# A two-layer kernel with per-sample weights and adapters: when the second layer's weight sums, adapters and next weights are made

## The chip, the cores and the metric

The kernel runs on one core of one Trainium2 chip. The time is device microseconds from launch to end, as the chip reports it for that core. The profile adds one traced execution. Its span, from the first to the last instruction, is somewhat shorter than the time of the same execution. Engines: PE (matmul), PEld (weight loads of PE), DVE (VectorE), ACT (ScalarE), POOL (GpSimd), and SP, which here only issues DMAs. DMAs are also issued from the queues of ACT and POOL.

## The reference

The input x is 8 batches of 256 tokens with 1024 features, in float32. Two layers follow, each with a residual.

```
# layer 1: per batch b a 0/1 mask of 1024 x 1024 and a coefficient c[b]
x = x + (x @ W0.T + b0) + (x @ (2*mask[b] - 1)) * c[b]
# layer 2: per batch b one of 24 adapters, rank 16, scaling 2
x = x + (x @ W1.T + b1) + 2 * (x @ A[itok[b]]) @ B[itok[b]]
```

## The kernel before, in words

**Layer 1.** A batch's effective weight is W0.T + 2c*mask - c, with the identity added for the residual. It is made in pieces of 128 x 1024 float32, eight to a batch, numbered k = 8b + i. `load(k)` issues the DMA of the mask (512 KB) and, for half of the pieces, of an x tile (256 KB) on SP's queue (L203, L207). `build(k)` expands the mask on ACT (L231) and adds W0 on DVE (L234). Batches 0 to 2 multiply the pieces directly (L292, L267). Batches 3 to 7 (`Seven`) cut weights and tokens into halves and do seven products in place of eight. `operands` makes the pieces, the weight sums s1 to s4 (L345) and the token sums t1 to t4 (L362); `products` multiplies (L408), adds the bias on ACT (L423) and accumulates quarters on DVE (L428). Its banks X, Y and Z are PSUM tiles.

**Layer 2.** It works on groups of four batches, and `second_layer` runs once after batch 3 and once after batch 7. The seven-product scheme is used at two levels. The outer products are A11, A12, S1, S2, S4, S3 and A22, in this order (`plan`), and `run` does one. Each has seven inner products with the leaves a11, s1, s2, a12, s3, a22 and s4 of 256 KB (L695). A leaf is read from DRAM by SP (L685) into one of seven buffers, each as soon as a buffer is free. The tiles e1 and e5 hold outer products that are needed twice, and c11, c12, c21 and c22 are the output quarters. `read` takes a finished bank out of PSUM: with a seed by a DVE add (L750), without one by an ACT copy (L749). The products A11 and S1 have no seed, so they are the ones that use ACT copies. ACT's queue also issues the stores of the output (L754). The adapters come in as `down` (L730, into h_sb), and `up` (L713, banks G), copied out by ACT (L723).

**W1's leaves.** W1 is loaded as 16 tiles of 256 KB (`raw`). `combine_weights` makes the sums of A11, A12, S1 and so on out of them in batches 2 and 3, by DVE, and `keep` (L514) stores each leaf to DRAM from POOL's queue. What doesn't fit then is left as generators in `later`: A22's four inner sums (L552 to L558), S2's four, S4's four, made in place (L575), and S3, which first reads two quarters back from DRAM on POOL's queue (`again`, L594, eight DMAs), then makes four outer sums (L586) and four inner ones in place. In batch 3 the hook `mid`, after the product s1, starts the adapters (`begin_adapters`: two DVE copies, two POOL memsets, eight DMAs on POOL's queue; `load_adapters`: another DVE copy and eight DMAs), then makes A22's sums and issues the stores of three of S4's quarters. The hook `late`, after s3, makes S2's sums. S4's and S3's sums come in the second layer.

**What sets the order.** A planner orders each engine's instructions when the program is built. It follows the order of the program, but by its own estimate of times it lets an instruction that is ready go ahead of an earlier one that is not. On the chip every engine then works through its list in that order. `behind(name)` restricts the planner: an instruction in its block is placed after the one kept as `anchors[name]`, if it runs on the same engine. "reads" is the last DVE read of a bank, "leaves" the last leaf load on SP, "weights" the last weight sum, "rows" the last adapter DMA on POOL. `run` takes a generator `beside` of small DVE steps (one step at each of four points, the rest at its end): the token sums of later products, the left weight sums, and, in group 0, the first pieces of batch 4 (`next_weights`, through `begin`). `next_masks(n)` issues the loads of batch 4's first n pieces.

**Buffers.** "w" has six tiles of 512 KB (pieces of even batches and of batch 1, the sums of A22 and S2, S3's A21), "q" ten (W1's quarters, e and c tiles), "l" seven (the leaves).

Of the kernel before, what the change touches and what calls it, by code (L numbers as in the profile page):

```python
# [24 lines left out]
def kernel(  # L25
# [38 lines left out]
    nc = tc.nc  # L64
# [105 lines left out]
    def load(k: int):  # L170

        b, h, g = pieces[k]

        if b in SEVEN and k % (2 * NG) >= 6 and b >= GB:
            pool, tag = qpool, "q"
        elif b in SEVEN and b % 2 and k % (2 * NG) < 6:
            pool, tag = tpool, "T"
        else:  # L180
            pool, tag = wpool, "w"
        weff[k] = pool.tile([P, CG, OH], F32, tag=tag, name=f"w_{k}")
        last = (k + 1) % (GB * 2 * NG) == 0
        pairs = [(weff[k].bitcast(I32), mask[b, g if b == 0 else h * NG + g])]
        if b == 0:
            pairs.append((w0_of(k), w0T[g]))
        x_pair = g // CG if b == 0 and g % CG == 0 else g if h == 0 else None
        if x_pair is not None:
            x = x_sb[b, x_pair] = xpool.tile([P, CG, T], F32, tag=f"x{x_pair}", name=f"x_{b}_{x_pair}")
        if k < BY_HALF:  # L190

            for i in range(2):
                for t, a in pairs:
                    nc.sync.dma_start(t[:, i], part(a, i))  # L194
                if k == 0 and i == 0:
                    nc.scalar.dma_start(x[:, 0], part(xT[0, 0], 0))
                elif k == 0:
                    nc.sync.dma_start(x[:, 1], part(xT[0, 0], 1))
                elif x_pair is not None and i == 0:
                    nc.sync.dma_start(x, xT[b, x_pair])  # L200
        else:
            for t, a in pairs:
                sent = nc.sync.dma_start(t, a)  # L203
            if last:
                anchors["masks"] = sent
            if x_pair is not None:
                nc.sync.dma_start(x, xT[b, x_pair])  # L207
        if k == NG:
            nc.sync.dma_start(b0_sb, b0)
        if k == 2 * NG:  # L210
            nc.sync.dma_start(itok_sb, itok)
        for n, (q, r) in enumerate(W1_ORDER):
            if k == 0 and r % 2 == 0:
                two = pair(f"w1_{q}_{r // 2}")
                raw[q, r], raw[q, r + 1] = two[:, 0], two[:, 1]
            if k == 2 * NG + n // 2:
                nc.sync.dma_start(raw[q, r], w1T[q, r])

    def build(k: int):
# [98 lines left out]
    class Seven:  # L318
# [3 lines left out]
        def __init__(self, b: int):  # L322
            self.b = b
            self.w, self.t = {}, {}
            self.ps = {}
            self.mid = self.late = lambda: None

        def block(self, i, j, a):

# [87 lines left out]
        def out(self, i, v):  # L417
            return self.y[i][:, :, v * H : (v + 1) * H]

        def with_bias(self, i, v, ps):  # L420
            for j in range(TPH):
                ot = i * TPH + j
                nc.scalar.activation(  # L423
                    self.out(i, v)[:, j, :], ps[:, j, :], AF.Identity, bias=b0_sb[:, ot : ot + 1]
                )
# [4 lines left out]
        def products(self):  # L430

            ps = self.ps
            for a in range(2):
                self.half("X", "a11", (0, 0), a, first=True)
                yield
            self.with_bias(0, 0, ps["X"])
            for a in range(2):
                self.half("Y", "a12", (1, 0), a, first=True)
                yield

            with behind("weights") if self.b < GB else nullcontext():
                self.add(0, 0, ps["Y"])
            for a in range(2):
                self.half("X", "s2", "t2", a)
                yield
            self.with_bias(0, 1, ps["X"])
            for a in range(2):
                self.half("Z", "s1", "t1", a, first=True)
                yield
            self.with_bias(1, 1, ps["Z"])  # L450
            self.mid()
            for a in range(2):
                self.half("X", "s3", "t3", a)
                yield
            self.add(1, 1, ps["X"])
            self.late()
            for a in range(2):
                self.half("Z", "s4", (1, 1), a)
                yield
            self.add(0, 1, ps["Z"])  # L460
            for a in range(2):
                self.half("X", "a22", "t4", a)
                yield
            self.with_bias(1, 0, ps["X"])
# [5 lines left out]
    def behind(what: str):  # L470
        return tc.issue_after(anchors[what].ins) if what in anchors else nullcontext()

    class Sevens:
# [6 lines left out]

        def begin(self, early: int):
            while self.made < early:
                with behind("reads"):
                    next(self.operands, None)
                self.made += 1

# [31 lines left out]
    def combine_weights():  # L518
# [17 lines left out]
        def inner(name, blocks, own, spare=False):  # L536


            a11, a12, a21, a22 = (blocks[u, v] for u in range(2) for v in range(2))
            for n, t in (("a11", a11), ("a12", a12), ("a22", a22)):  # L540
                if n in own:
                    keep(name, n, t)
            s = {}
            for n in ("s1", "s2", "s3", "s4"):
                if not spare:
                    s[n] = lpool.tile([P, CG, OQ], F32, tag="l", name=f"{name}_{n}")
                else:
                    if n in ("s1", "s3"):
                        half = wpool.tile([P, 2, CG, OQ], F32, tag="w", name=f"{name}_{n}")
                    s[n] = half[:, n in ("s2", "s4")]  # L550
                if n == "s1":
                    nc.vector.tensor_add(s[n], a21, a22)  # L552
                elif n == "s2":
                    nc.vector.tensor_sub(s[n], s["s1"], a11)
                elif n == "s3":
                    nc.vector.tensor_sub(s[n], a11, a21)
                else:
                    nc.vector.tensor_sub(s[n], a12, s["s2"])  # L558
                keep(name, n, s[n])
                yield  # L560
# [112 lines left out]
    def second_layer(group: int, y, first, first_steps, second):  # L673
# [72 lines left out]

        def read(out, ps, other=None):
            if other is None:
                return nc.scalar.copy(out, ps)  # L749
            own["reads"] = anchors["reads"] = nc.vector.tensor_add(out, ps, other)  # L750
            return anchors["reads"]

# [101 lines left out]
                if group + 1 < NGROUP:  # L854
                    load_to((group + 1) * GB * 2 * NG + n)

        def next_weights():
            for n in range(3 if group + 1 < NGROUP else 0):
                sevens[group + 1].begin(n + 1)
                yield  # L860


        def ordered(steps):
# [5 lines left out]
                yield  # L869

        own = {}
        left = {n: ordered(later[n] if group == 0 else iter(())) for n in ("S3", "S4")}
        with behind("masks"):
            load_leaves("A11")
        begin(0, "A11", first)
        for _ in ordered(first_steps):
# [3 lines left out]
        lower = (c11, c12)  # L880
        run(
            0, "A11", first, None, e1,
            beside=chain(ordered(second.sums()), islice(left["S3"], 1), islice(t1, 2), left["S4"]),
            early=down,
            mid=lambda: up(0, 0, lower),
            late=lambda: up(0, 1, lower),
# [2 lines left out]
        for uv in UV[1:]:  # L889
            add(c11[uv], e1[uv])  # L890
        t2 = ordered(outer_sum(2, b22, big_t[1], "S2"))
        run(
            1, "A12", second, c11, c11,
            dest=(0, 0),
            beside=chain(t1, islice(left["S3"], 4), islice(t2, 2)),
        )
        next_masks(4)
        e5 = quads("e5")
        run(
            2, "S1", right["S1"], None, e5,  # L900
            beside=chain(t2, ordered(right["S4"].sums()), left["S3"]),
            then=lambda uv: add(c12[uv], e5[uv]),
        )
        run(
# [6 lines left out]
        run(  # L911
            4, "S4", right["S4"], c12, c12,
            dest=(0, 1),
            beside=ordered(outer_sum(4, b21, big_t[2], "A22")),
            mid=lambda: up(1, 0, upper),
            late=lambda: up(1, 1, upper),
        )
# [5 lines left out]
                    add(c22[uv], e5[uv])  # L923
                yield

        nonlocal limit
        limit = n_pieces
        run(5, "S3", right["S3"], e1, e1, beside=chain(next_weights(), add_e5()), then=lambda uv: add(c21[uv], e1[uv]))


        next_masks(6)
# [5 lines left out]
                yield  # L937

        run(6, "A22", right["A22"], c21, c21, dest=(1, 0), beside=last_quarter())


    load_to(LOADS_AHEAD)
# [8 lines left out]
    def step(k: int):  # L951

        nonlocal sums
        if k == 2 * NG + 1:
            sums = combine_weights()
        with tc.issue_after(weff_at[min(k + BUILDS_AHEAD, max(weff_at))].ins):
            for _ in range(3):
# [5 lines left out]
    for group in range(NGROUP):  # L963
# [18 lines left out]
        if group == 0:  # L982
# [3 lines left out]
            for _ in sums:  # L986
                pass

            def mid(late=y[GB - 1][1][:, 0, H : H + 1]):
                with behind("weights"):  # L990
                    begin_adapters(late)
                    load_adapters(0, late)
                sums_of("A22")
                with behind("rows"):
                    next(later["S4"])

            def sums_of(name):
                with behind("weights"), behind("rows"):
                    for _ in later[name]:
                        pass  # L1000

            sevens[0].batches[-1].mid = mid
            sevens[0].batches[-1].late = lambda: sums_of("S2")
        sevens[group].run(y, between)
        anchors["layer"] = anchors["weights"]
        second_layer(group, y, first, first_steps, second)
# [72 lines left out]
```

## Time and profile before

| | us |
|---|---|
| time, median of 3 runs | 417.87 (416.04, 417.87, 525.24) |
| time of the profiled execution | 416.53 |
| its span | 414.4 |
| PE busy | 403.4 (97%) |
| DVE busy | 312.0 (75%) |
| ACT busy | 137.5 (33%) |
| POOL busy | 42.8 (10%) |
| DMA | 99.55 MB, 240 GB/s on the mean |

The stages by PE in the trace: batch 3 from 90.4 to 115.4 us, group 0's second layer from 115.4 to 217.4, batches 4 to 7 from 217 to 317.3 (their first matmuls are mixed into A22's), and group 1's second layer from 317.3 to the end. The table's shares are means over stages with different limits. A line of the timeline reads: start, length, engine, line, operation, output<-input, shapes, count, and in brackets how long the engine was idle before and what ended that. A line of the waits reads: who waited for whom, us in total, how often, the longest.

### The profile page before, as it was taken

The page shows a single profiled execution, that of the slowest core. Times are in us where ns is not written, and L with a number is a line of the kernel's source. Part 1 is how long each engine was busy: PE and PEld are TensorE (multiplying, and loading weights), DVE is VectorE, ACT ScalarE, POOL GpSimd, SP SyncE. Part 2 cuts the span into 40 slices and gives each one's busy share as a digit, 9 for nine tenths or more (in the row PEclk, how much of TensorE's full clock was granted, in tenths as well). Part 3 has the DMA queues.
Part 4 walks back from the last instruction along what each step waited for, and adds up shares of the span by engine and source line. Part 5 has one row for each costly group of instructions (what it writes and reads, how often), then busy time and mean ns, then how long its engine had stood idle before and what let it go on. Part 6 is the DMA issues. An engine that isn't in the chain of part 4 may idle for free.

```text
span 414.4 us, 6761 instructions
## 1 busy us (share of the span) xinstructions
PE 403.4 (97%) x2554; PEld 358.7 (87%) x2554; DVE 312.0 (75%) x446; ACT 137.5 (33%) x221; POOL 42.8 (10%) x85
## 2 busy tenths in 40 slices
PE   8999999999999978999998999999999999999996
PEld 6888888899977866888888999999999788888885
DVE  3357598889704985997999999999922177898593
ACT  4443434872134105013037864732221420101100
POOL 0000252000784210200000000300000000000000
PEclk9999999999999998999999999999999999999999
DMA  8999999960389999766699857732113247655654
GB/s 289 405 402 395 402 412 418 408 269 2 98 294 365 320 315 405 242 195 226 209 358 396 317 160 251 272 121 58 27 52 74 80 127 236 171 154 158 220 156 152
DMA packets 42403, 99.55 MB, mean 240 GB/s; under 512 B 5636, under 2 KB 6404, under 8 KB 42372
## 3 DMA queue, kind: packets, MB, share of 16 engines
q1 hardware_dynamic: 32690, 76.17, 53.3%
q0 software_dynamic: 4928, 14.71, 9.5%
q10 hardware_dynamic: 4754, 8.26, 5.4%
q8 instruction: 20, 0.33, 0.3%
q14 instruction: 11, 0.09, 0.1%
HBM read 79.19 MB, written 19.92 MB: 239 GB/s over the span
## 4 chain that ended last, share of the span: by engine, by line
PE 90%; DMA 4%; DVE 2%; ACT 1%; issue 1%; SPq 1%; DVEq 0%; ACTq 0%
PE X L695 24%; PE X L408 17%; PE ps L267 12%; PE Z L695 11%; PE Z L408 9%; PE Y L695 5%; PE ps L292 4%; PE Y L408 3%; PE G L713 2%; PE psh L730 2%; DMA outT<-c 2%; DMA w_sb<-w0T 2%; DMA w<-mask 1%; DVE w L234 1%; SPq L194 1%
## 5 line engine op out<-in xcount | busy, mean ns | idle before, releaser
L231 ACT ACTIVATE w<-w,neg_c,two_c 128x1024 f32<-128x1024 int32 (+1 forms) x67 | 79.9, 1203 | 72.6 <-DMA w<-mask 45.8
L234 DVE TENSOR_TENSOR w<-w,w_sb 128x1024 f32<-128x1024 f32 (+1 forms) x67 | 77.3, 1172 | 24.6 <-ACT w L231 21.3
L267 PE MATMUL ps<-x,w 128*128 128x256 f32 x256 | 55.7, 379 | 0.3 <-DVE w L234 0.3
L267 PEld LDWEIGHTS ps<-x,w 128*128 128x128 f32 x256 | 48.6, 190 | 7.2 <-DVE w L234 0.7
L423 ACT ACTIVATE y<-X,b_sb 128x128 f32<-128x128 f32 x60 | 17.1, 367 | 61.8 <-PE X L408 60.5
L833 DVE TENSOR_TENSOR c<-c,e 128x512 f32<-128x512 f32 x48 | 31.9, 684 | 5.4 <-ACT c L723 4.6
L408 PE MATMUL X<-t,s 128*128 128x128 f32 x288 | 33.9, 275 | 1.1 <-ACT y L423 1.1
L723 ACT COPY c<-G 128x512 f32<-128x512 f32 x32 | 16.4, 600 | 54.7 <-PE G L713 54.7
L408 PEld LDWEIGHTS X<-t,s 128*128 128x128 f32 x288 | 33.0, 192 | 1.3 <-ACT y L423 1.3
L292 PE MATMUL ps<-x,w 128*128 128x256 f32 x128 | 28.2, 381 | 0.5 <-DVE w L234 0.5
L292 PEld LDWEIGHTS ps<-x,w 128*128 128x128 f32 x128 | 24.3, 191 | 4.6 <-DVE w L234 1.2
L695 PE MATMUL X<-T_t,l_S_s 128*128 128x256 f32 x96 | 24.4, 399 | 3.2 <-ACT e L749 3.2
L750 DVE TENSOR_TENSOR e<-Y,e 128x512 f32<-128x512 f32 x8 | 5.5, 689 | 27.5 <-PE Y L695 15.7
L695 PEld LDWEIGHTS X<-T_t,l_S_s 128*128 128x128 f32 x96 | 19.1, 201 | 6.8 <-ACT e L749 3.6
L408 PE MATMUL X<-t,w 128*128 128x128 f32 x192 | 22.4, 275 | 0.0
L408 PEld LDWEIGHTS X<-t,w 128*128 128x128 f32 x192 | 21.9, 192 | 0.0
L749 ACT COPY e<-X 128x512 f32<-128x512 f32 x16 | 9.4, 586 | 37.6 <-PE X L695 28.7
L345 DVE TENSOR_TENSOR s<-w,w 128x1024 f32<-128x1024 f32 x18 | 21.6, 1218 | 0.1
L750 DVE TENSOR_TENSOR c<-X,c 128x512 f32<-128x512 f32 (+1 forms) x26 | 16.6, 646 | 6.7 <-PE X L695 6.6
L408 PE MATMUL X<-x,w 128*128 128x128 f32 x160 | 19.0, 275 | 0.0
L408 PEld LDWEIGHTS X<-x,w 128*128 128x128 f32 x160 | 18.7, 192 | 0.2
L408 PE MATMUL Z<-t,s 128*128 128x128 f32 x160 | 18.8, 275 | 0.0
(144 smaller groups left out, 661.4 us busy)
## 6 DMA issues: line engine op xcount, KB each, us to landing
w<-mask SPq DMA_DIRECT2D x61, 512.0 KB, 7.2
l_S_s<-leaf_S_s SPq DMA_DIRECT2D x32, 256.0 KB, 2.8
x<-xT SPq DMA_DIRECT2D x31, 256.0 KB, 7.6
outT<-c ACTq DMA_DIRECT2D x30, 256.0 KB, 3.2
l_A_s<-leaf_A_s SPq DMA_DIRECT2D x24, 256.0 KB, 2.7
l_S_a<-leaf_S_a SPq DMA_DIRECT2D x24, 256.0 KB, 2.9
w<-w1T SPq DMA_DIRECT2D x16, 256.0 KB, 6.6
leaf_A_s<-A_s POOLq DMA_DIRECT2D x12, 256.0 KB, 6.1
```

The source lines that it names most:

```text
L231: nc.scalar.activation(w[:, i], m[:, i], AF.Identity, bias=neg_c[:, b : b + 1], scale=two_c[:, b : b + 1])
L234: weff_at[k] = nc.vector.tensor_add(w[:, i], w[:, i], w0_of(k)[:, i])
L267: nc.tensor.matmul(ps[j // 2][:, j % 2, :], lhsT=w[:, c, j * P : (j + 1) * P], rhs=x_sb[b, g][:, c, :],  start=first and j % 2 == 0, stop= ...
L292: nc.tensor.matmul(ps[ot // 2][:, ot % 2, :], lhsT=w[:, h, j * P : (j + 1) * P], rhs=x_sb[0, c // CG][:, c % CG, :], start=c == 0 and ot % ...
L345: anchors["weights"] = op(s, self.w[x, a], self.w[y, a])
L408: anchors["products"] = nc.tensor.matmul(ps[:, j, :], lhsT=w[:, c, j * P : (j + 1) * P], rhs=r, start=first and a == 0 and c == 0 and j == ...
L423: nc.scalar.activation(self.out(i, v)[:, j, :], ps[:, j, :], AF.Identity, bias=b0_sb[:, ot : ot + 1])
L695: anchors["inner"] = nc.tensor.matmul(ps[:, j, :], lhsT=l[:, c, j * P : (j + 1) * P], rhs=r[:, c, :], start=first and c == 0 and j == 0, s ...
L723: nc.scalar.copy(dest[b // 2][u, b % 2], ps[b])
L749: return nc.scalar.copy(out, ps)
L750: own["reads"] = anchors["reads"] = nc.vector.tensor_add(out, ps, other)
L833: nc.vector.tensor_add(o, o, x)
```

## The change

There are five edits.

1. W1's sixteen loads go out at a rate of 1.5 to a piece instead of 2, and `combine_weights` starts one piece later.
2. The two hooks of batch 3 become four, at the products 1, 5, 7 and 3 (in their order of execution). After product 1 come the adapters and the stores of the quarters of S2 and S4, after 5 A22's sums, after 7 S2's, and after 3, behind the add of s4, S4's.
3. In the second layer S4's sums are gone. S3's reads come at the first free point of A11, its outer sums at the end of A11 and its inner ones in A12. The second operand's sums move back by one point.
4. The loads of batch 4's first four pieces are issued before A12, not after it.
5. The first pieces of batch 4 are made in S1 (two), S4 (the third) and S3 (the fourth), not in S3 (three), and `begin` puts their mask expansions behind the last ACT copy. `limit`, which lets these steps load further pieces, is raised after A22 and not before S3.

```diff
-            if k == 2 * NG + n // 2:
+            if k == 2 * NG + 2 * n // 3:
                 nc.sync.dma_start(raw[q, r], w1T[q, r])
...
-            self.mid = self.late = lambda: None
+            self.after = {}
...
+        def read(self, n):
+            if n in self.after:
+                self.after[n]()
...
             self.with_bias(0, 0, ps["X"])
+            self.read(1)
...
             self.with_bias(1, 1, ps["Z"])
-            self.mid()
+            self.read(5)
...
             self.add(1, 1, ps["X"])
-            self.late()
+            self.read(7)
...
             self.add(0, 1, ps["Z"])
+            self.read(3)
...
-                with behind("reads"):
+                with behind("reads"), behind("copies"):
                     next(self.operands, None)
...
             for n, t in (("a11", a11), ("a12", a12), ("a22", a22)):
                 if n in own:
                     keep(name, n, t)
+            if own and spare:
+                yield
...
             if other is None:
-                return nc.scalar.copy(out, ps)
+                anchors["copies"] = nc.scalar.copy(out, ps)
+                return anchors["copies"]
...
-        def next_weights():
-            for n in range(3 if group + 1 < NGROUP else 0):
-                sevens[group + 1].begin(n + 1)
-                yield
+        def next_weights(n):
+            if group + 1 < NGROUP:
+                while sevens[group + 1].made < n:
+                    sevens[group + 1].begin(sevens[group + 1].made + 1)
+                    yield
...
-        left = {n: ordered(later[n] if group == 0 else iter(())) for n in ("S3", "S4")}
+        s3 = ordered(later["S3"] if group == 0 else iter(()))
...
             0, "A11", first, None, e1,
-            beside=chain(ordered(second.sums()), islice(left["S3"], 1), islice(t1, 2), left["S4"]),
+            beside=chain(islice(s3, 1), ordered(second.sums()), islice(s3, 4), islice(t1, 2)),
...
         t2 = ordered(outer_sum(2, b22, big_t[1], "S2"))
+        next_masks(4)
         run(
             1, "A12", second, c11, c11,
             dest=(0, 0),
-            beside=chain(t1, islice(left["S3"], 4), islice(t2, 2)),
+            beside=chain(t1, s3, islice(t2, 2)),
         )
-        next_masks(4)
...
-            beside=chain(t2, ordered(right["S4"].sums()), left["S3"]),
+            beside=chain(t2, ordered(right["S4"].sums()), next_weights(2)),
...
-            beside=ordered(outer_sum(4, b21, big_t[2], "A22")),
+            beside=chain(ordered(outer_sum(4, b21, big_t[2], "A22")), next_weights(3)),
...
-        nonlocal limit
-        limit = n_pieces
-        run(5, "S3", right["S3"], e1, e1, beside=chain(next_weights(), add_e5()), then=lambda uv: add(c21[uv], e1[uv]))
+        run(5, "S3", right["S3"], e1, e1, beside=chain(add_e5(), next_weights(4)), then=lambda uv: add(c21[uv], e1[uv]))
...
         run(6, "A22", right["A22"], c21, c21, dest=(1, 0), beside=last_quarter())
+        nonlocal limit
+        limit = n_pieces
...
-        if k == 2 * NG + 1:
+        if k == 2 * NG + 2:
             sums = combine_weights()
...
-            def mid(late=y[GB - 1][1][:, 0, H : H + 1]):
+            def adapters(late=y[GB - 2][1][:, 0, :1]):
                 with behind("weights"):
                     begin_adapters(late)
                     load_adapters(0, late)
-                sums_of("A22")
+
                 with behind("rows"):
-                    next(later["S4"])
+                    for name in ("S2", "S4"):
+                        next(later[name])
...
-            sevens[0].batches[-1].mid = mid
-            sevens[0].batches[-1].late = lambda: sums_of("S2")
+            sevens[0].batches[-1].after = {
+                1: adapters,
+                5: lambda: sums_of("A22"),
+                7: lambda: sums_of("S2"),
+                3: lambda: sums_of("S4"),
+            }
```

## The prediction, made before the changed kernel was built or run

> **What bounds the kernel now.** I read the page first, then who waited for whom on PE, then the instructions in order of time around the one large wait, and last the stretches of both groups beside each other.
>
> ```profile
> PE 90%; DMA 4%; DVE 2%; ACT 1%; issue 1%; SPq 1%; DVEq 0%; ACTq 0%
> ```
>
> ```profile
> PE X L695 <- ACT e L749: 3.8, 2, 3.2
> ...
> PE X L408 <- ACT y L423: 1.1, 1, 1.1
> ```
>
> PE is the bound: it carries 90% of the chain, and after the start (first weights, 17.09 us) it waits only twice for long. So any gain is bounded. The two groups do the same second layer, and group 1 shows it undisturbed: there the low-rank products G of A11's second half begin at 334.44 us and those of S4 at 378.88, 44.44 apart; in group 0 at 132.57 and 183.87, 51.30 apart. Group 0 loses 51.30 - 44.44 = 6.86 us, nearly all in S1. With the 1.1 us at batch 4's start, about 8 us can be won in all: 2% of 416.53, no more.
>
> Where the 6.86 go, in order of time:
>
> ```profile
> 147.69 0.33 SPq L203 DMA_DIRECT2D w<-mask  x1
> ...
> 154.61 1.24 ACT L231 ACTIVATE w<-w,neg_c,two_c 128x1024 f32<-128x1024 int32 x1 [9.46 <-DMA outT<-c]
> ...
> 155.76 0.56 ACT L749 COPY e<-X 128x512 f32<-128x512 f32 x1
> ...
> 156.38 3.50 PE L695 MATMUL X<-T_t,l_S_s 128*128 128x256 f32 x8 [3.16 <-ACT e L749]
> ```
>
> A mask of batch 4 is issued at 147.69 and takes 6.8 us to land (transfers of that moment), so at 154.5. Its expansion stands in ACT's queue ahead of the copy of S1's second quarter, whose product ended at 151.5 (149.60 + 1.89). So the copy waits for the mask, and PE for the copy. The releaser named is a store, but the mask's landing fits to 0.1 us. A second expansion does the same at 158.31. PE then runs 8 matmuls in 3.50 us instead of 1.89.
>
> ```profile
> 154.00:160.00 6.00, 3.50 (x8) 2.50 (x8) 2.70 (x5) 3.03 (x4) 0.00 (x0) 0.72 1.03 412
> 160.00:166.00 6.00, 5.35 (x24) 4.44 (x25) 4.69 (x8) 3.46 (x4) 0.00 (x0) 1.00 1.04 395
> ```
>
> Columns: stretch, length, busy PE, PEld, DVE, ACT, POOL, PE clock, DMA share, GB/s. The clock fell to 0.72 after the pause, and DMA is full (412 and 395 GB/s).
>
> **What the Trainium skill says.** "TensorE: Matmul & The Clock Gate", part 1: after an idle window of some 3.4 us PE's clock halves until it has been busy as long again. The trace agrees: 3.16 us of pause, clock 0.72, 1.61 us of slow matmuls; a pause of 1.14 us at 224.13 shows none. "DMA: Bandwidth & Descriptors", Queues, rings and completion order: transfers of one issuing queue are taken up in ring order, and the engines alternate between queues. The trace agrees: the leaf issued at 155.71 behind the masks took 8.5 us, against 3.2 for the leaves of S1 in group 1. "GPSIMD Engine Reference", Specifications: POOL shares SBUF ports with VectorE when that reads two SBUF inputs. Before, the two memsets (106.15) ran beside an idle DVE, so no run shows their cost beside sums.
>
> **Part by part.** *W1's loads.* The 16 loads of 256 KB go 1.5 to a piece, not 2, and the sums start a piece later. Bytes are the same, and DMA is full there (413 GB/s in 62 to 83 us). The last quarter is issued at piece 21 and summed at step 20 of the sums, piece 24: 3 x 3.46 us (16 matmuls of 0.216) = 10.4 us, landing 6.6. Slack 3.8 us; cost 0, between -0.3 and +1.
>
> *Batch 3.* Three DVE copies (0.45 us), two memsets (0.97 + 0.31), 16 adapter DMA issues (107.41 to 115.92, 8.5 us) and 6 stores of S2 and S4 (3.3 us) go from about 106 to about 94.6. DMA moves 4 GB/s in 90.4 to 104, so they cost no bandwidth. DVE is busy 13.56 of 13.60 us there. The tightest sum, S2's second half, ends at 98.15, and its matmuls come halfway in the product of 97.41, at 99.2: slack 1 us covers 0.45. If the memsets hold the DVE for their whole 1.28 us, 0.7 us is left over. I take 0, range 0 to 0.7. POOL's queue ends about 12 us sooner: 94.6 + 1.3 + 8.5 + 3.3 = 107.7, then 12 stores and S3's 8 loads of 0.55, so about 121 against 132.7.
>
> S4's four sums (0.69 each, 138.5 to 142.8) go behind the add at 111.90. DVE then idles 11.83 us until 126.22, so they are free. This also ends the wait of the copy at 144.57, held for a buffer until a store of S4 had landed, 1.9 us after its product.
>
> *S3's sums.* The second operand's t1 to t3 move one slot later; t4 and S3's four outer sums now stand ahead of S1's T. T began at 136.22; with 5 x 0.60 it begins at 139.2, and its first half is done at 140.4. PE wants it at 140.70. Cost 0 to 1; I take 0.3. The reloaded quarters land by 121 + 8.2 = 129, in time. In A12 four inner sums stand where four outer ones did: equal. S1 and S2 lose 8 sums (4.9 us) and take two weight adds (2 x 1.22).
>
> *Masks earlier.* This is the new risk. Four masks and four x tiles (4 x 512 + 4 x 256 KB, 3.15 MB) now go on SP's queue between A12's last leaf and S1's first.
>
> ```profile
> 132.60 0.32 SPq L685 DMA_DIRECT2D l_A_s<-leaf_A_s  x1
> 135.60 0.32 SPq L685 DMA_DIRECT2D l_S_a<-leaf_S_a  x1
> ...
> 140.70 1.97 PE L695 MATMUL X<-T,l_S_a 128*128 128x256 f32 x8
> ```
>
> S1's first leaf had about 5 us from issue to use. Behind 3.15 MB plus its own 0.26 and A12's last 0.26 it lands no sooner than 132.6 + 2.0 (a quiet landing of 2.7 less 0.65 of data) + 3.67/0.41 = 143.5: PE waits 2.8 us. If other queues keep 40% of the engines, as in 130 to 165 us before (SP 60.1%), it is 132.6 + 2 + 14.9 = 149.5: 8.8 us and 1.6 of slow clock. Much of that traffic is now earlier: 18 stores or loads of 256 KB (4.7 MB) leave the stretch after 116 us. Below zero it can't go. If PE's order puts a product of A12 (1.73 us) ahead, 1.1 is left. I take 3.0; ends 1.0 and 10.4. Queued behind the masks on SP are all seven leaves of S1, but they follow at 0.65 us each while PE uses one in 1.73.
>
> *Expansions.* They are now behind the copies. The first two come at S1's end, ACT's next copies are G's at 184 (20.82 us idle before), so a late mask holds nobody. That returns the 6.86 us. Their two DVE adds fall into S2, where group 1's DVE is busy 11.36 of 12.1 us. Before, S3's four inner sums (2.4 us) stood there, as long, at a loss of some 0.4 us that remains. The third and fourth go into S4 and S3, which sheds two of three adds. I put the DVE's loss at 0.4, from 0 to 1.8 (one read kept back by two adds).
>
> *Batch 4's start.* Its fifth mask goes from 190.79 to about 204, behind A22's leaves, and moves the sixth by 0.52/0.4 = 1.3 us; the sixth's add waited for DVE from 210 to 216.16, so that is covered. DVE loses two adds and gains one between 205 and 217. Of the 1.1 us stall I count 0.5 won; between -1.5 and +1.
>
> Sum: -6.86 + 3.0 + 0.3 + 0.4 - 0.5 = -3.7 us. The profiled execution took 416.53 (span 414.4, 2.1 around it), 1.3 below the median of 417.87. Forecast 416.53 - 3.7 = **412.8 us**, span 410.7.
>
> **Rivals.** (1) *The leaves come in time* (another order on SP or PE, or faster transfers): no wait at S1's start, 416.53 - 6.86 - 1.1 = 408.6. For it: DMA is unloaded from 116 us on. Against it: 3.67 MB in 8 us leave nothing over. (2) *The wait only moves, and grows*: slower than before. S1's first leaf stands behind the masks as in the lower bound above: 416.53 - 6.86 + 10.4 = 420.1. The place is SP's queue after 132.6; it decides as soon as the leaf lands later than about 147. For it: the leaf behind the masks before landed 16.5 us after the first mask was issued. Passing 2% needs PE waiting until about 157, which a mask held on SP for a weight buffer would do; six buffers less S3's two are just the four needed, free once S2's stores land (by about 120). (3) *The planner still sets the expansions ahead*, or DVE's order takes back what ACT's gives: 415 to 418, 416.5.
>
> **How the numbers follow.** Forecast (410.5 to 414.5) 0.58; rival 1 0.12; rival 2 0.17, of which 0.07 over 2%; rival 3 0.13. Two per cent, about what a measurement of this kernel can tell from no change, is 8.4 us: 409.5 and 426.2. Faster by more: half of rival 1, 0.06. Slower by more: rival 2's tail and what I haven't seen, 0.09. Within: 0.85. The range, 409 to 420, leaves out half of rival 1 and rival 2's tail.
>
> **What would show it.** In the changed kernel: no PE wait on ACT's copies in S1; masks on SP right after A12's last leaf; a PE wait of 1 to 5 us before S1's first product, put down to that leaf's transfer; weight expansions after S1's last copy; S4's stores done before 120 us; G of A11's second half to G of S4 some 48 us. Wrong would be: the wait at S1's first product over 7 us or absent, DVE's reads in S2 holding PE for more than 2 us, or PE waiting in batch 3.

## The result, and the profile after

The changed kernel takes 420.67 us (median of 22 runs, 418.52 to 424.72), the kernel before 417.63 us beside it (22 runs). The ratio is 1.007 with a 95% interval of [1.0047, 1.0094]: 0.7% slower, within the 2% that I had set as the bound of no change, but on the other side of it than forecast, and just above my range of 409 to 420. Medians here are of all executions; ratios leave out those that took over 1.5% more than the fastest of the same kernel. The profiled execution took 420.91 us (span 419.2), 4.38 us more than that of before. It is my second rival that came about, the wait that only moves and grows.

The page's chain, PE's waits, and the part of the chain around the largest of them, in that order:

```profile
PE 77%; DMA 12%; DVE 6%; SPq 1%; ACT 1%; issue 1%; DVEq 0%; ACTq 0%
```

```profile
PE X L703 <- DMA l_S_a<-leaf_S_a: 7.2, 1, 7.2
PE X L408 <- ACT y L427: 1.9, 1, 1.9
```

```profile
135.43 1.33 SPq L203
...
136.81 0.74 SPq L207
...
137.65 9.68 DMA l_S_a<-leaf_S_a
147.33 0.14 issue
147.46 8.28 PE X L703 x24
```

DMA's share of the chain has gone from 4% to 12%. That is not the size of the loss: only 2.3% of the span is this leaf, and 6.8% are loads of masks, most of them at batch 4's start (207 to 233 us), where PE waits no more than the 1.9 us above. PE no longer waits for ACT's copies in S1: both of those waits are gone. In their place stands one wait of 7.2 us, for one leaf. (L703 of this kernel is L695 of before, L693 the leaf's load, L757 and L759 the two reads of a bank, L721 the low-rank product.)

The timeline shows how it comes about. First SP, then PE, then ACT:

```profile
132.11 0.32 SPq L693 DMA_DIRECT2D l_A_s<-leaf_A_s  x1
132.60 0.33 SPq L203 DMA_DIRECT2D w<-mask  x1
...
136.81 0.74 SPq L207 DMA_DIRECT2D x<-xT  x1
137.65 0.54 SPq L693 DMA_DIRECT2D l_S_a<-leaf_S_a  x1
```

```profile
138.37 1.89 PE L703 MATMUL Y<-y,l_A_a 128*128 128x256 f32 x8
147.46 1.19 PE L703 MATMUL X<-T,l_S_a 128*128 128x256 f32 x2 [7.20 <-DMA l_S_a<-leaf_S_a]
148.45 3.62 PE L703 MATMUL X<-b_t,l_A_s 128*128 128x256 f32 x8
151.86 2.15 PE L703 MATMUL X<-T,l_S_a 128*128 128x256 f32 x6
153.85 1.89 PE L703 MATMUL X<-b_t,l_A_a 128*128 128x256 f32 x8
```

```profile
167.87 0.59 ACT L757 COPY e<-X 128x512 f32<-128x512 f32 x1 [2.87 <-PE X L703]
168.35 4.64 ACT L231 ACTIVATE w<-w,neg_c,two_c 128x1024 f32<-128x1024 int32 x4
```

SP issues the four masks and x tiles right after A12's last leaf, as the diff says. S1's first leaf follows them at 137.65, 2.05 us later than before (135.60), and takes 9.68 us to land. PE is ready for it at 140.1. After the pause PE's clock is low: the 16 matmuls from 147.46 to 153.85 take 6.4 us where 3.45 is their time at full clock (8 in 1.73 us), so 2.95 us more are lost. All expansions stand behind S1's last copy.

Windows of the changed kernel, columns as in the prediction:

```profile
133.00:140.10 7.10, 7.10 (x36) 6.00 (x32) 6.27 (x10) 2.05 (x4) 1.64 (x3) 1.00 0.92 304
140.10:147.30 7.20, 0.16 (x1) 0.00 (x0) 3.99 (x6) 0.00 (x0) 0.00 (x0) 0.70 1.02 399
147.30:156.00 8.70, 8.54 (x26) 7.08 (x27) 2.20 (x4) 0.59 (x1) 0.00 (x0) 0.66 0.37 95
```

In the wait DMA is full (share 1.02, 399 GB/s). From one low-rank product G to the other, A11's second half to S4's first, the changed kernel takes 187.11 - 132.01 = 55.10 us; before it was 51.30, in group 1 44.44. Its excess is 55.10 - 44.44 = 10.66 = 7.20 (wait) + 2.95 (clock) + 0.5 (rest). It had been 6.86.

### The profile page after: what moved, and what is told of

Its sections match the earlier page's. It is cut to its first block, busy times and chain, and to the rows that moved or that the text cites. A ratio compares the mean times of both kernels' runs of the same rounds, so it can differ in the third digit from the quotient of the medians.

```text
span 419.2 us, 6762 instructions
## 1 busy us (share of the span) xinstructions
PE 404.0 (96%) x2554; PEld 360.7 (86%) x2554; DVE 312.1 (74%) x446; ACT 136.6 (33%) x221; POOL 43.0 (10%) x85
## 4 chain that ended last, share of the span: by engine, by line
PE 77%; DMA 12%; DVE 6%; SPq 1%; ACT 1%; issue 1%; DVEq 0%; ACTq 0%
PE X L703 19%; PE X L408 14%; PE ps L267 13%; PE Z L703 8%; PE Z L408 8%; DMA w<-mask 7%; PE ps L292 4%; PE Y L703 4%; PE Y L408 3%; DMA l_S_a<-leaf_S_a 2%; PE G L721 2%; PE psh L738 2%; DMA w_sb<-w0T 2%; DMA outT<-c 2%; DVE c L842 1%; DVE e L759 1%
## 5 line engine op out<-in xcount | busy, mean ns | idle before, releaser
L231 ACT ACTIVATE w<-w,neg_c,two_c 128x1024 f32<-128x1024 int32 (+1 forms) x67 | 78.9, 1203 | 67.2 <-DMA w<-mask 55.4
L757 ACT COPY e<-X 128x512 f32<-128x512 f32 x16 | 9.4, 588 | 58.9 <-PE X L703 52.6
L759 DVE TENSOR_TENSOR c<-X,c 128x512 f32<-128x512 f32 (+1 forms) x26 | 16.6, 646 | 16.1 <-PE X L703 16.0
L759 DVE TENSOR_TENSOR e<-Y,e 128x512 f32<-128x512 f32 x8 | 5.5, 689 | 25.8 <-PE Y L703 14.0
L703 PE MATMUL X<-T_t,l_S_s 128*128 128x256 f32 x96 | 22.8, 380 | 0.1
L703 PEld LDWEIGHTS X<-T_t,l_S_s 128*128 128x128 f32 x96 | 18.2, 190 | 2.9 <-DVE e L759 0.5
L703 PE MATMUL X<-T,l_S_a 128*128 128x256 f32 x48 | 12.8, 410 | 7.2 <-DMA l_S_a<-leaf_S_a 7.2
L408 PE MATMUL Y<-x,w 128*128 128x128 f32 x160 | 18.7, 275 | 0.0
```

What stands on the lines that cost most here:

```text
L231: nc.scalar.activation(w[:, i], m[:, i], AF.Identity, bias=neg_c[:, b : b + 1], scale=two_c[:, b : b + 1])
L408: anchors["products"] = nc.tensor.matmul(ps[:, j, :], lhsT=w[:, c, j * P : (j + 1) * P], rhs=r, start=first and a == 0 and c == 0 and j == ...
L703: anchors["inner"] = nc.tensor.matmul(ps[:, j, :], lhsT=l[:, c, j * P : (j + 1) * P], rhs=r[:, c, :], start=first and c == 0 and j == 0, s ...
L757: anchors["copies"] = nc.scalar.copy(out, ps)
```

## The experiments

My theory after the result: the masks' 3.15 MB cost PE about 10 us wherever they stand in SP's queue ahead of a leaf that is needed within some 5 us, and the move alone explains the loss. The rivals: (a) another of the five edits costs the time (POOL's or DVE's new order); (b) it is bandwidth and not the queue, so another queue would not help; (c) the ACT order was the true gain, and the move of the masks spoiled it. All kernels below compute the full result. Ratios are to the kernel before, run beside each, with their 95% intervals.

**The masks put back (e1), and the masks moved alone (e2).**

```diff
 e1, from the changed kernel
-        next_masks(4)
         run(1, "A12", second, c11, c11, ...)
+        next_masks(4)
 e2, from the kernel before
+        next_masks(4)
         run(1, "A12", second, c11, c11, ...)
-        next_masks(4)
```

> The changed kernel with one part undone: batch 4's four masks and x tiles go out after A12 again, all else stays. If S1's first leaf was late because it stood behind them on SP's queue, PE's wait of 7.2 us ahead of S1's first product and the slow clock behind it go. The same 3.15 MB then stand ahead of S2's first leaf, which PE wants at about 154.4: sent from 147.2 it can't land before 147.2 + 2 + 3.67/0.41 = 158, so a wait of 3 to 6 us appears there, and the time is 415 to 418. If the leaf was late for the load of all the DMA engines, and the place in SP's queue matters little, the wait only disappears: 409 to 412.

> The kernel before with this one part of the change alone: the masks and x tiles of batch 4 ahead of A12. By SP's queue: PE waits 6 to 10 us ahead of S1's first product (DMA is fuller there than in the changed kernel), the wait on ACT's copy in S1 goes since the masks are there, and the time is 419 to 424. If what costs in the changed kernel is another of its parts, this one is level with the kernel before or faster: 411 to 418.

e2 took 421.68 us, 1.0104 [1.0054, 1.0155]. PE's waits of e2:

```profile
PE X L695 <- DMA l_S_a<-leaf_S_a: 6.9, 1, 6.9
PE X L695 <- DVE c L750: 2.0, 2, 1.5
```

So this one edit is enough for the whole loss without the other four, and rival (a) isn't needed for it. The wait in e2 is less clean than in the changed kernel, though. Batch 4's fourth piece is not made through `begin` there, so nothing keeps it back, and its weight add stood in DVE's queue for 7.08 us, until 151.26, with the reads of two banks behind it. The leaf landed at the same moment (issued at 141.69, 9.54 us), so had the leaf come sooner, PE would probably have waited for these reads.

But e1, with it undone, is no faster: 421.56 us, 1.0100 [1.0051, 1.0150]. S1 starts on time (140.78), and then the wait stands elsewhere. PE in e1:

```profile
158.87 1.13 PE L703 MATMUL Z<-T,l_S_s 128*128 128x256 f32 x4 [0.62 <-DVE e L759]
165.69 3.75 PE L703 MATMUL X<-T,l_S_a 128*128 128x256 f32 x8 [5.69 <-DMA l_S_a<-leaf_S_a]
```

The masks now begin at 147.22, S2's first leaf is issued behind them at 158.01, and PE waits 5.69 us for it, with a slow clock after. Neither place on SP's queue is free of it. The wait at S2's first leaf had been expected (3 to 6 us); the time had not (415 to 418). What the other four edits are worth by themselves stays open: e1 has them all and stands at 1.0100, the next run has one of them alone and stands at 1.0028.

**Only the expansions behind the copies (e5).**

```diff
 from the kernel before
-                with behind("reads"):
+                with behind("reads"), behind("copies"):
...
+                anchors["copies"] = nc.scalar.copy(out, ps)
+                return anchors["copies"]
```

> The kernel before with one other part of the change alone: the four mask expansions of batch 4 stand behind S1's last ACT copy; the masks go out where they did, after A12. My forecast counted the whole 6.86 us of S1 as returned by this. If the wait for the masks was all that stood there, PE runs through S1 and the time is 409 to 412. If the leaf of S2, which landed at 164.2 in the kernel before just as PE came to it, was the next limit behind it, PE's wait only changes its name: it stands ahead of S2's first product, 4 to 6 us on that leaf's transfer, with a slow clock after it, and the time is 415 to 420.

418.54 us, 1.0028 [1.0011, 1.0045]: a little slower, not faster. (Only the three pieces that this kernel makes through `begin` are bound by the edit; the fourth came after the copies by itself. The traced execution, 420.99 us, is one of the slowest of 20.) PE in e5:

```profile
156.12 1.99 PE L695 MATMUL X<-T_t,l_S_a 128*128 128x256 f32 x8 [0.68 <-ACT e L749]
157.95 1.91 PE L695 MATMUL Z<-T,l_S_s 128*128 128x256 f32 x8
164.17 3.75 PE L695 MATMUL X<-T,l_S_a 128*128 128x256 f32 x8 [4.32 <-DMA l_S_a<-leaf_S_a]
```

The wait for ACT that I had read as the loss is nearly gone (0.68 us are left of it), and behind it stands the leaf, issued at 155.34 after the masks. In the kernel before the same leaf was issued at 155.71 and took 8.5 us, to 164.2; PE, held up by ACT, came to it late enough. So the 6.86 us were not to be had from ACT's order alone. Rival (c) falls.

**The masks in two halves (e3).**

```diff
 from the changed kernel
-        next_masks(4)
+        next_masks(2)
         run(1, "A12", second, c11, c11, ...)
+        next_masks(4)
```

> The changed kernel with two masks and their x tiles ahead of A12 and the other two after it. By SP's queue half the bytes stand ahead of S1's first leaf: it lands at 132.6 + 2 + 2.1/0.41 = 139.7 at best, so PE waits 0 to 3 us there, and as long or less at S2's first leaf; without a pause of 3 us the clock stays up. 410 to 414. If each place costs a wait whatever stands there, 418 to 421.

420.82 us, 1.0107 [1.0047, 1.0166], a miss. PE waits 0.65 us at S1's first leaf but still 3.58 at S2's, and its next 8 matmuls take 3.61 us. Half the masks, 1.57 MB, suffice for that. The waits on leaves come to 4.2 us against 7.2 and the slow clock behind them to 1.7 against 2.95, yet the time is the same. Of the 4.2 us won so, 1.1 goes to a wait for DVE in S4. Another 1.6 goes to a second slow clock at batch 4's start. PE waits for ACT's y there in both kernels, 1.94 us in e3 and 1.88 in the changed kernel, but the 32 matmuls that follow take 5.46 us in e3 and 3.84 in the changed kernel. PE's chain, first of e3, then of the changed kernel:

```profile
233.85 5.46 PE X L408 x32
```

```profile
235.30 3.84 PE X L408 x32
```

The planner also ordered PE's products otherwise in e3. Some 1.5 us stay open.

**Fewer bytes in the same place (e6), and the same bytes on ACT's queue (e4).** e6 sends the masks alone before A12, and the x tiles behind S1's leaves. e4 sends the same masks and tiles from ACT's queue at nearly the same moment (131.90 to 142.18).

```diff
 e6: in load, and behind "leaves" after A12
-            if x_pair is not None:
+            if x_pair is not None and b == GB:
+                held.append((x, xT[b, x_pair]))
+            elif x_pair is not None:
...
+            for x, at in held:
+                nc.sync.dma_start(x, at)
 e4: load and load_to take a queue
-        next_masks(4)
+        next_masks(4, nc.scalar)
```

> The changed kernel with the four masks at their place and the four x tiles behind S1's leaves, so 2.1 MB and not 3.15 stand ahead of S1's first leaf. By the order of SP's queue it lands 1.05 / 0.4 = 2.6 us sooner: PE waits 3.5 to 5.5 us ahead of S1's first product, not 7.2; and 1 MB ahead of S2's first leaf costs 0 to 2 us. 416 to 420. If the number of bytes doesn't matter, the wait stays at 6.5 to 8 us and the time at 420 to 422.

> The changed kernel with the same four masks and x tiles sent at the same point from ACT's queue, behind ACT's last copy of A11, and not from SP's: the same bytes at the same time on the same engines, but S1's leaves no longer stand behind them. If the order within SP's queue is the cause, PE waits at most 1.5 us ahead of S1's first product: 410 to 414. If the load of the engines is the cause, the leaf lands as late as before and PE waits 5 to 8 us: 418 to 421.

e6: 417.91 us, 0.9984 [0.9957, 1.0011]. e4: 417.33 us, 1.0012 [0.9988, 1.0037]. PE at S1's first product, first in e6, then in e4:

```profile
144.05 1.97 PE L707 MATMUL X<-T,l_S_a 128*128 128x256 f32 x8 [2.77 <-DMA l_S_a<-leaf_S_a]
```

```profile
142.29 1.97 PE L703 MATMUL X<-T,l_S_a 128*128 128x256 f32 x8 [2.33 <-DMA l_S_a<-leaf_S_a]
144.86 1.10 PE L703 MATMUL Z<-T_t,l_S_s 128*128 128x256 f32 x4 [0.61 <-DMA l_S_s<-leaf_S_s]
```

1.05 MB less ahead of the leaf shortens the wait by 7.20 - 2.77 = 4.4 us, more than the forecast 2.6. The same bytes on another queue shorten it by 7.20 - 2.33 - 0.61 = 4.3 us: the leaf is issued at 134.81, not held up behind eight issues, and lands within 7.5 us. That is between the two expectations (a wait of at most 1.5 us, or of 5 to 8). So a place behind the masks in the same queue is what most of the wait comes of, and sharing the engines makes the rest: rival (b) is true of the smaller part. The two are not wholly parted, as ACT's queue also spreads the bytes: between 132 and 142 us it moved 2.27 of the 3.15 MB. In both traces the 8 matmuls after the wait take 1.97 us, with no slow clock. That does not hold for every execution: e4's trace is the fastest of its 20. The six executions with a mean granted clock of 1.000 took 415.23 to 416.70 us, the five at 0.991 or less 420.18 to 423.66. So e4's median pays in part for a clock that falls in some executions and not in others; after which pause it fell there isn't recorded.

**The masks earlier, from POOL's queue (e7).** The stores of S2 and S4 are earlier in the changed kernel, so POOL's queue is empty from 124.2. e7 puts the masks there, right behind S3's reads.

```diff
 from e4
+                anchors["reloads"] = nc.gpsimd.dma_start(t, at)
...
-            with behind("leaves"), behind("copies"):
+            with behind("leaves"), behind("reloads"):
...
-        next_masks(4, nc.scalar)
+        next_masks(4, nc.gpsimd)
```

> The changed kernel with the four masks and x tiles sent from POOL's queue, behind S3's eight reloads: eight us sooner (about 124 to 129) and beside SP's queue, so that no leaf stands behind them and their bytes are through by about 136. By the order of the queue and the load of that moment PE waits at most 0.7 us at S1's first and S2's first product: 409 to 413. If 3.15 MB ahead of S1 cost PE the same wherever they are sent, 416 to 420.

414.23 us, 0.9922 [0.9894, 0.9951], faster than both kernels, if not as fast as expected. All seven executions have a mean clock of 0.999 or 1.000. Windows of e7:

```profile
125.00:133.00 8.00, 8.00 (x51) 6.31 (x53) 4.47 (x7) 2.95 (x7) 4.36 (x8) 1.00 1.03 395
133.00:141.00 8.00, 8.00 (x48) 6.50 (x44) 6.40 (x10) 2.53 (x5) 1.63 (x3) 1.00 1.03 394
```

Between 125 and 133 us the changed kernel moved 280 GB/s; here it is 395. The masks use that room, and SP's leaf is not behind them. PE waits 1.56 us at S1's first product.

**The same from the kernel before (e10).** Is it POOL alone, or does it need the earlier stores of batch 3?

```diff
 from e5, with the queue and "reloads" of e7
+        next_masks(4, nc.gpsimd)
         run(1, "A12", second, c11, c11, ...)
-        next_masks(4)
```

> The kernel before with two things alone: the expansions behind S1's ACT copies, and the masks and x tiles of batch 4 sent from POOL's queue before A12. Batch 3, S4's and S3's sums are as before. If the part of the change that moves stores and sums into batch 3 is worth something, it is by the emptier DMA engines at S1's start: here the leaf of S1 shares full engines, PE waits 1 to 4 us there and the time is 414 to 418, behind the 414.2 of the changed kernel with the same queue. If that part is worth nothing, level with it: 413 to 415.

422.01 us, 1.0091 [1.0056, 1.0127], slower than either expectation. PE's waits of e10, then DVE and PE around the longest of them:

```profile
PE X L695 <- DVE c L751: 8.4, 3, 4.2
```

```profile
153.17 1.22 DVE L234 TENSOR_TENSOR w<-w,w_sb 128x1024 f32<-128x1024 f32 x1 [8.83 <-ACT w L231]
```

```profile
155.05 3.38 PE L695 MATMUL X<-b_t,l_A_a 128*128 128x256 f32 x8 [4.17 <-DVE c L751]
```

Here POOL's queue holds stores and S3's reads until 139.5 (the last read is issued at 138.98), the planner mixes masks and reads, and the fourth mask is issued only at 142.92. DVE stands 8.83 us before a weight add that needs this mask, and the reads of two banks stand behind the add, so PE waits 4.17 us. The edit did not prevent it: as in e2, the fourth piece is not made through `begin`, and its expansion (at 151.90) runs ahead of S1's first copy (153.69). The changed kernel makes all four pieces through `begin`. Against e7 e10 is 1.7% or some 7 us slower, and this wait with the slow clock behind it (3.38 us for 8 matmuls) is a large part of that. So e10 shows that POOL's queue is not enough by itself, but not how much the emptier queue of the changed kernel is worth: the stores, the mixed order and the free fourth piece aren't separated.

**DVE's order on top of e7 (e8, e9).** e8 puts S1's T ahead of S3's outer sums. e9 also takes the adds of batch 4's first two pieces out of S1 and S2.

```diff
 e8, from e7
-            beside=chain(islice(s3, 1), ordered(second.sums()), islice(s3, 4), islice(t1, 2)),
+            beside=chain(islice(s3, 1), ordered(second.sums()), islice(t1, 2), islice(s3, 4)),
 e9, from e8
-            beside=chain(t2, ordered(right["S4"].sums()), next_weights(2)),
+            beside=chain(t2, ordered(right["S4"].sums())),
...
-            beside=chain(ordered(outer_sum(4, b21, big_t[2], "A22")), next_weights(3)),
+            beside=chain(ordered(outer_sum(4, b21, big_t[2], "A22")), next_weights(2)),
```

> The kernel with the masks on POOL's queue, with one more step: S1's two T sums stand ahead of S3's four outer sums on DVE, not behind them. There PE waited 1.56 us ahead of S1's first product on a DVE instruction that ended at 142.46, the first after the T sums. If S3's sums ahead of T are the cause, T is done 2.4 us sooner, this wait goes to 0.3 or less and the time falls by 0.5 to 1.5 us: 412.5 to 414. If the leaf is what came last there (it landed at about 141.6), 0.5 to 1 us of wait stays. If DVE only hands the 2.4 us on to the reads of A12, the time stays at 414 to 415.

> As the last, and the two weight adds of batch 4 that stand in S2's time (2.36 us on DVE, right after S1) move to S4, the other two to S3. The prediction put DVE's loss there at 0.4 us, 0 to 1.8. If the two adds hold S2's and S4's reads back, PE's wait of 1.1 us on DVE at S4 goes and the time falls by 1 to 2 us: 411 to 413. If DVE's total load is what binds, the wait comes back in S3 or A22, and the time stays within 0.5 us.

e8: 413.78 us, 0.9910 [0.9878, 0.9941], no different from e7 by its interval. T is done at 138.7 instead of 141.9, and PE still waits 1.72 us at S1's first product, now put down to the leaf; so in e7 too the leaf was about as late as T. e9: 411.07 us, 0.9850 [0.9811, 0.9888], the best version. PE's waits, first of e8, then of e9:

```profile
PE X L703 <- DMA l_S_a<-leaf_S_a: 1.7, 1, 1.7
...
PE X L408 <- ACT y L427: 1.3, 1, 1.3
PE X L703 <- DVE c L759: 1.1, 1, 1.1
```

```profile
PE X L703 <- DMA l_S_a<-leaf_S_a: 1.8, 1, 1.8
...
PE X L408 <- ACT y L427: 0.9, 1, 0.9
```

The wait of 1.1 us on a DVE read in S4 is gone with the two adds, as expected; from e8 to e9 the profiled execution falls by 413.64 - 411.38 = 2.26 us.

**The masks later, from POOL's queue (e11).** With e9's order, the masks go behind S3's last store (156.89 to 162.6).

```diff
 from e9
-            with behind("leaves"), behind("reloads"):
+            with behind("leaves"), behind("kept"):
...
-        next_masks(4, nc.gpsimd)
         run(1, "A12", ...)
         ...
         run(2, "S1", ...)
+        next_masks(4, nc.gpsimd)
```

> As the last but one (masks on POOL's queue, T first, the weight adds in S4 and S3), and the four masks and x tiles go out from POOL's queue behind S3's last store, at about 160 us, not at 125 to 132. There S1's first leaf still came 1.8 us late, with the masks' bytes and the reloads filling the engines (395 GB/s). If that load was the cause, the wait goes to 0.4 or less, and since DMA moves 153 GB/s in 166 to 175 us and the adds come only in S4, the masks' new place costs nothing: 409 to 411. If S2's and S4's leaves then suffer as S1's did, 1 to 3 us of PE's wait come back there: 411 to 414.

417.70 us, 1.0018 [0.9989, 1.0046], a miss. S1 starts on time (140.43), and the wait stands at S4's first leaf, issued at 160.55. PE in e11:

```profile
162.08 1.89 PE L703 MATMUL Y<-T,l_S_a 128*128 128x256 f32 x8
167.80 2.90 PE L703 MATMUL X<-y,l_S_a 128*128 128x256 f32 x6 [3.83 <-DMA l_S_a<-leaf_S_a]
170.49 3.40 PE L703 MATMUL X<-T_t,l_S_s 128*128 128x256 f32 x8
```

Even on another queue, 3.15 MB cost PE 3.83 us and a slow clock when they start a few us ahead of a leaf that PE is about to need. What e7 to e9 win comes of the queue and of the moment together. Two variants near these were not run: the masks on SP's own queue at e7's early moment, and S1's first leaf issued on SP ahead of the masks.

## Why the prediction was wrong, by its own steps

**The step that failed is "I take 3.0" for S1's first leaf**: it measured 10.15 us (7.20 of wait, 2.95 of slow clock). Its mechanism and place were right, and the landing, 147.33, lies between the bounds 143.5 and 149.5; I chose near the lower one, since 4.7 MB had left the stretch after 116 us. (Rival 2 names the lower bound, but its 10.4 is that of the later landing, 149.5.) That traffic had indeed gone, but other bytes took its place. From 132.6 to 147.4 DMA moved 5.08 MB: 4.22 on SP's queue, since the leaves issued behind S1's first one shared the engines with it, and 0.79 on POOL's, S3's stores. I had counted 3.67. With 5.08 MB my own sum gives 132.6 + 2.0 + 5.08/0.41 = 147.0. As these bytes are counted up to the landing itself, that shows what filled the time; it is no forecast. The slow clock I had only in the upper end, and too small there (1.6). "The Trainium skill", "DMA: Bandwidth & Descriptors", Queues, rings and completion order, has each engine alternate between the queues that have work for it; e4 agrees, with the leaf landing in 7.5 us instead of 9.68 and 2.8 us earlier in the queue.

**"That returns the 6.86 us"** held, but only beside the moved masks. With this edit alone (e5) S2's leaf comes too late and nothing is won. I had quoted that leaf's 8.5 us and not asked when PE would want it once ACT no longer held it up.

**Batch 3**, 0 (0 to 0.7): right. PE has no wait there, and the DVE sum beside the first memset took as long as always. DVE and POOL of the changed kernel:

```profile
94.81 1.22 DVE L345 TENSOR_TENSOR s<-w,w 128x1024 f32<-128x1024 f32 x1
```

```profile
94.82 0.97 POOL L125 MEMSET lb_pad<- 128x1024 f32 x1 [23.37 <-DVE h_sb L124]
```

The stores of S4 were issued by 117.2 and POOL's queue ended at 124.2 against a forecast of about 121.

**W1's loads**, 0: batch 3's product Y starts at 93.34 against 93.83. I can't tell the 0.5 us from scatter: no run undoes this edit alone, and e1 with the same loads has Y at 93.85, as before.

**S3's sums**, 0.3: T began at 138.73, forecast 139.2, and its first half was done at 139.9, in time for 140.1. **DVE in S2**, 0.4: together with T some 0.5 (the rest in the excess above). With the leaf out of the way these two adds cost more, 2.26 us from e8 to e9, beyond my upper end of 1.8; PE's products were also ordered differently there, so not all of it need be the adds.

**Batch 4's start**, -0.5: it went the other way, +0.7 (from S4's first G to batch 5's first Y 61.87 us before, 62.58 after, and the wait for ACT's y 1.1 to 1.9), within its ends of -1.5 and +1.

The sum: forecast -3.7, measured +4.38, a difference of 8.1. Of it 10.15 - 3.0 = 7.15 is S1's leaf and 0.7 + 0.5 = 1.2 batch 4's start; the rest cancels within 0.3. So the misjudged size explains nearly all. Of the marks to look for, G to G was forecast at 48 and came to 55.1, and "the wait at S1's first product over 7 us", named as what would make it wrong, is what happened. I gave rival 2 a chance of 0.17; its bound for the wait, taken as seriously as the choice of 3.0, should have had more.

## What to carry to other kernels

When a stall is removed, look for what the trace has standing behind it: here an ACT wait covered a late leaf, and each place for the same 3.15 MB on the one load queue cost PE 7 to 10 us of wait and slow clock (e1, e2, e5 and the changed kernel). For a small load that is needed soon, count every byte that is put in flight before it lands, those of later loads and other queues too, and add a pause's slow clock to it. Prefetch belongs in a stretch where the engines have room, on a queue where nothing urgent is behind it (e7: 395 GB/s in place of 280, no wait of PE over 1.6 us after its start). And when loads move, look at which instructions are free to go ahead of others: in e2 and e10 the weight add of one piece, which nothing kept back, stood in DVE's queue ahead of the reads that PE needed.

## What the runs showed of the hardware

A leaf of 256 KB lands in 2.6 to 3.2 us on the median of a kind of leaf over the changed kernel's run. It took at most 7.5 us while the masks came from ACT's queue at the same time (e4), and 9.7 us behind them on its own queue.

The clock after a pause of PE isn't given by the pause's length alone. A pause of 2.77 us (e6) was followed by clock 1.00, one of 2.67 (e10) by 0.57:

```profile
144.00:148.00 4.00, 3.95 (x18) 3.53 (x19) 1.10 (x2) 0.59 (x1) 0.00 (x0) 1.00 0.79 226
```

```profile
143.80:147.00 3.20, 3.20 (x9) 2.55 (x10) 0.54 (x1) 0.00 (x0) 1.09 (x2) 0.57 1.04 389
```

Still shorter pauses did it: 1.94 us in e3 (shown above), and 1.82 us at batch 4's start in e5. There 16 matmuls took 3.30 us; in the kernel before, after a pause of 1.14 us at the same place, they took 2.05. The chain in e5:

```profile
226.96 3.30 PE X L408 x16
```

After the kernels' start, every pause of 3.16 us and more was followed by a slow clock (before, e1, e2, e3, e5, e10, e11 and the changed kernel), and none under 1.8 us was. The loss is 1.5 to 3 us for each. The Trainium skill, "TensorE: Matmul & The Clock Gate", part 1, has the clock fall after an idle window of some 3.4 us and says that the window runs freely. The length does not fit these traces, where less was enough, the 3.16 us of the prediction included; that where a pause falls counts does fit, though no run here shows the window itself.

The one POOL memset of 0.97 us that ran beside a DVE sum of two inputs didn't lengthen the sum: 1.22 us, as without it (changed kernel, 94.81).
